# Row scores spread through DRAM, dense jobs paced beside expert pairs, and three norms finished alone

## The chip, the cores and the metric

One core of a Trainium2 chip runs the kernel. The metric is device time in microseconds: the median of the runs of one kernel, each from launch to the end. A profiled execution gives the trace; its span runs from the first to the last instruction.

## The reference, cut to what matters

The input x is 64 batches (graphs) of 256 nodes with 256 features, float32, with one adjacency matrix for all. Two layers follow each other; each is a graph attention and then a feed-forward part, each on the normalised input and added to it:

```python
x = x + elu(gat(layernorm(x), adj, W0, a0))        # 4 heads of 64, slope 0.2
x = x + layernorm(x) @ wf.T + bf
x = x + relu(gat(layernorm(x), adj, W1, a1))       # 1 head of 256, slope 0.01
x = x + moe(layernorm(x))                          # 8 experts, the best 2 of each row

# gat, for one head:
e[i, j] = leaky_relu(s[i] + d[j]);  e[i, j] = -big where adj[i, j] == 0
out = softmax(e) @ h
# moe: logits = t @ router.T; t + sum over the best 2 of weight * (gelu(t @ w1[e] + b1[e]) @ w2[e] + b2[e])
```

The kernel computes exp(leaky_relu(s + d)) as a maximum of two products of exponentials, so an attention matrix costs one VectorE instruction a tile once three numbers a node are known. One of these three is wanted along the free axis, for all partitions alike: the **row terms**. They are found by node on partitions, so they have to be turned and spread.

## The kernel before, in words

**Batches.** `batch_layers` (L594) is a Python generator for one batch; nodes lie on the partitions in two tiles (NT = 2) of 128. It computes the first norm, the first attention, the linear layer, the second attention and the last norm, and the routing logits. Every `yield r` ends its work for this step and gives its rank in the next step; `yield -r` puts it back in the same step at rank r.

**Steps.** The loop at L1241 writes out the whole program in steps. A step takes all active generators from a heap by rank; what they issue stands in that order on each engine's queue. So the order on every engine is fixed when the program is written, and the engines run it in order. A new batch begins every third step (TICKS = 3), so some seven batches are under way at once, each at another place. A step costs no time by itself: it is only an order.

**Row terms of the first attention** (from batch 1 on): `send_terms` (L533) turns them with VectorE (L537), `terms_queue(b).dma_start` (L621) writes 4 KB to DRAM, `spread_terms` (L552, issue at L554) reads them back into all partitions (512 KB), and `scores` (L570) uses them two steps later. The queue is SyncE's (SP) from batch 18 (SETTLED) on.

**Row terms of the second attention**: `projected1` (L497) computes the exponentials `ex` on ScalarE (L511); one step later, at rank 25, `scores1` (L520) has TensorE turn and spread them by two transposes into a PSUM bank `pd` (L523), and VectorE forms the two tiles of `z` (L528). A step after that, at rank 40, `attended` (L576) multiplies (L584).

**Norms.** `norm_stats` (L366) lets VectorE compute means and variances (L378, L379). Two such norms of one step share one finish: the second call does it, or, where there is only one, the end of the step (L1277). `finish_norms` (L399) runs on GpSimd (add, power; L406, L407), and from step 3 * 66 = 198 on (`at_end`) on VectorE, in 11 small instructions (L387 to L404). The norms of the last batches have no partner, for no new batch is loaded.

**Experts.** Batches 0 to 60 are routed: their rows are sent by GpSimd's indirect DMAs (L1066) into regions by expert. A **pair** is 256 rows of one expert. `expert_pair` (L890) loads it (L906 to L935), turns it, computes `hidden` (L964) and `result` (L990), scales it (ScalarE, L961), and `scatter` (L998) adds it to the output by two indirect DMAs of GpSimd (L1004). The two of one pair wait until the two of the pair before have landed (`before`, L1001). There are 129 pairs; from step 165 (SINGLE_AT) on at most one begins in a step.

**Dense jobs.** Batches 61, 62 and 63 are not routed; every expert is applied to all of their rows (`dense_expert`, L1022), in two groups: batch 61 (8 jobs of 1 unit), batches 62 and 63 (8 jobs of 2 units). A unit is one batch under one expert: `hidden` and `product`, then four VectorE instructions (L1036). `dense_free` (L1258 to L1261) spaces the jobs: a job of n units keeps the next one off for n steps. `store_dense` (L1043) writes a batch out when its last job is done.

**Queues.** GpSimd's queue carries the sends, the scatters and the finishes of norms. SP carries all loads, the stores and the row terms. Buffers that bound the run-ahead: 5 of `xr`, 7 of `we` (pairs and dense jobs together), 9 of `y`, 8 PSUM banks, 1 of `z1`.

Of the kernel before, what the change touches and what calls it, by code (L numbers as in the profile page):

```python
# [9 lines left out]
F32 = mybir.dt.float32  # L10
I32 = mybir.dt.int32
AF = mybir.ActivationFunctionType
ALU = mybir.AluOpType
AX = mybir.AxisListType

P = 128
# [5 lines left out]
def rows_to_all(ap: bass.AP, n: int) -> bass.AP:  # L22

    return bass.AP(tensor=ap.tensor, offset=ap.offset, ap=[[0, P], [1, n]])
# [3 lines left out]
def kernel(  # L28
# [17 lines left out]
    nc = tc.nc  # L46
    B, N, D = x.shape
# [4 lines left out]
    NT = N // P  # L52
# [21 lines left out]
    work = ctx.enter_context(tc.tile_pool(name="work", bufs=2))  # L74
    small = ctx.enter_context(tc.tile_pool(name="small", bufs=4))
# [3 lines left out]
    def bank(name, shape):  # L79
        t = psum.tile([P, 2 * D], F32, tag="bank", name=name, bufs=8)  # L80
        n = 1
        for s in shape:
            n *= s
        t = t[:, :n]
        if len(shape) == 2:
            t = t.rearrange("p (a b) -> p a b", a=shape[0])
        elif len(shape) == 3:
            t = t.rearrange("p (a b c) -> p a b c", a=shape[0], b=shape[1])
        return t
# [22 lines left out]
    S = 32  # L112
    G = P // S
# [13 lines left out]
    AHEAD, BLOCKS_AHEAD = 3, 2  # L127
    PAIRED = CHUNKS[0] + CHUNKS[1] + 3
    SETTLED = CHUNKS[0] + CHUNKS[1] + CHUNKS[2] + CHUNKS[3] + 2


    ident = const.tile([P, P], F32, tag="ident", name="ident")
# [186 lines left out]
    def once(work):  # L319
# [14 lines left out]
        out=tri, in_=tri, pattern=[[1, P]], base=0, channel_multiplier=-1,  # L334
# [28 lines left out]
    SINGLE_AT = TICKS * (B - 9)  # L363
    order, order_steps = [], []

    def norm_stats(src):  # L366

        stats = small.tile([P, NT, 6], F32, tag="stats", name="stats")
        if half_done:
            mv, rstd = half_done[0]  # L370
            at = NT
        else:
            mv = small.tile([P, 2 * NT, 2], F32, tag="mv", name="mv", bufs=4)
            rstd = small.tile([P, 2 * NT], F32, tag="rstd", name="rstd", bufs=5)
            half_done.append((mv, rstd))
            at = 0
        for t in range(NT):
            nc.vector.bn_stats(stats[:, t, :], src[:, t, :])  # L378
            nc.vector.bn_aggr(mv[:, at + t, :], stats[:, t, :])  # L379
        if at:  # L380
            finish_norms(2 * NT)
        return mv[:, at : at + NT, :], rstd[:, at : at + NT]

    def at_end():
        return order_steps[-1] >= TICKS * (B + 2)

    def inverse_root(y, v):  # L387

        n = v.shape[-1]
        t = small.tile([P, 2 * NT], F32, tag="root", name="root", bufs=2)[:, :n]  # L390
        nc.vector.tensor_scalar(
            y.bitcast(I32), v.bitcast(I32), -0.5, float(0x5F3759DF), op0=ALU.mult, op1=ALU.add
        )
        for _ in range(3):
            nc.vector.tensor_tensor(t, y, y, ALU.mult)
            nc.vector.scalar_tensor_tensor(t, t, -0.5, v, op0=ALU.mult, op1=ALU.mult)
            nc.vector.scalar_tensor_tensor(y, t, 1.5, y, op0=ALU.add, op1=ALU.mult)

    def finish_norms(n):  # L399
        mv, rstd = half_done.pop()  # L400
        if at_end():
            var = small.tile([P, 2 * NT], F32, tag="sq", name="var", bufs=4)[:, :n]
            nc.vector.tensor_scalar(var, mv[:, :n, 1], EPS, None, op0=ALU.add)
            inverse_root(rstd[:, :n], var)  # L404
            return
        nc.gpsimd.tensor_scalar_add(rstd[:, :n], mv[:, :n, 1], EPS)  # L406
        nc.gpsimd.tensor_tensor(rstd[:, :n], rstd[:, :n], mhalf[:, :n], ALU.pow)  # L407
# [84 lines left out]
    for i in range(2):  # L492
        t = keep.tile([P, NT, D + 1], F32, tag=f"q1_{i}", name=f"q1_{i}")
# [23 lines left out]
            nc.scalar.activation(me[:, j, :], masks[1][:, j, :], AF.Copy, scale=ex[:, j, 0:1])  # L517
        return q, ex, me

    def scores1(ex, me):  # L520
        pd = bank("pd", [N])
        for t in range(NT):
            nc.tensor.transpose(  # L523
                pd[:, t * P : (t + 1) * P], ex[:, t, 1:2].to_broadcast([P, P]), ident
            )
        z = work.tile([P, NT, N], F32, tag="z1", name="z1", bufs=1)
        for j in range(NT):
            nc.vector.scalar_tensor_tensor(  # L528
                z[:, j, :], pd, ex[:, j, 2:3], me[:, j, :], op0=ALU.max, op1=ALU.mult
            )  # L530
        return [z[:, j, :] for j in range(NT)]

    def send_terms(q, b):  # L533


        ut = small.tile([P, S], F32, tag="ut", name="ut", bufs=1)
        nc.vector.transpose(  # L537
            ut.rearrange("p (t h w) -> p t h w", t=NT, h=H), q[:, :, :, HD - 1 : HD + 3]
        )
        ud = tc.dram_tile([S, S], F32, name=f"terms_{b}")  # L540
        ud = ud.rearrange("c r -> (c r)").rearrange("(c p) -> c p", p=P)
        return ut, ud
# [51 lines left out]
    def batch_layers(b, c0, xng, lg):  # L594

        def first_norm():
            x0 = xin.pop(b)
            if b + AHEAD < B:
                xin[b + AHEAD] = load_batch(b + AHEAD)
            return x0, norm_stats(x0)[1]  # L600

        if b:
            x0, rstd = first_norm()
# [8 lines left out]
        if not b:  # L612
            x0, rstd = first_norm()
# [4 lines left out]
        if b:  # L618
            ut, ud = send_terms(q, b)
            yield -31  # L620
            terms_queue(b).dma_start(  # L621
                out=ud.rearrange("c (g r) -> g c r", g=G),
                in_=ut[2 : P : S // (NT * H), :],
            )
            yield -52
        z = work.tile([P, NT, NT, H, P], F32, tag="z4", name="z4", bufs=2)
# [17 lines left out]
        ex = work.tile([P, NT, D], F32, tag="e", name="e", bufs=1)  # L644
        nc.scalar.activation(ex, hp, AF.Exp)

        x1 = work.tile([P, NT, D], F32, tag="x1", name="x1", bufs=1)
# [2 lines left out]
        x1b = work.tile([P, NT, D], F32, tag="x1b", name="x1b", bufs=1)  # L650
        nc.vector.tensor_add(x1b, x1, bias_f[:, None, :].to_broadcast([P, NT, D]))
        yield 21
        _, rstd = norm_stats(x1)
        yield -30
        xT = transposed(x1)
        yield 70
# [9 lines left out]
        for t in range(NT):  # L666
            nc.vector.scalar_tensor_tensor(  # L667
                x2[:, t, :], pf[:, t, :], rstd[:, t : t + 1], x1b[:, t, :],
                op0=ALU.mult, op1=ALU.add, accum_out=sums[:, t : t + 1],
            )  # L670
        yield 7
        rstd = norm_squares(x2, sums)
# [3 lines left out]
        xT = transposed(x2)  # L676
        yield 20
        q, ex, me = projected1(xT, rstd, b)
        yield 25
        z = scores1(ex, me)  # L680
        yield 40
        pvs, rinv = attended(
            q[:, :, None, :], 1, lambda j, h, t: z[j][:, t * P : (t + 1) * P]
# [9 lines left out]
        for t in range(NT):  # L693
            nc.vector.scalar_tensor_tensor(
                x2[:, t, :], x2[:, t, :], 1.0, rel[:, t, :],
                op0=ALU.mult, op1=ALU.add, accum_out=sums[:, t : t + 1],
            )
        yield 6
        rstd = norm_squares(x2, sums)
# [33 lines left out]
        if not dense:  # L733
            d = nc.sync.dma_start(
                out=out_rows[b * N : (b + 1) * N, :].rearrange("(t p) d -> p t d", p=P), in_=base
# [320 lines left out]
    active = []  # L1056
    waiting, dense_jobs = [], []
    sent = []

    def begin(job, rank):  # L1060
        active.append([rank, len(order), job])
        order.append(job)
# [172 lines left out]
    step, more, credit = 2, True, 0.0  # L1235


    SETUP_AT = 4
    dense_free = 0
    with tc.manual_schedule():  # L1240
        while more or active or waiting or dense_jobs or scatters:  # L1241
            phase = step % TICKS
            if more and (phase == 0 or step == 2):
                nxt = next(batches, None)
                more = nxt is not None
                if more:
                    begin(nxt, 40 if phase == 0 else 25)
            if step >= SETUP_AT and setup:
                begin(setup.pop(0)(), 90)
            if step >= SINGLE_AT:  # L1250
                if waiting and len(scatters) < 3:
                    begin(waiting.pop(0)(), 90)
            elif phase == 1:
                credit = min(credit + 3.0, 2.0)
                while waiting and credit >= 1.0:
                    credit -= 1.0
                    begin(waiting.pop(0)(), 90)
            if dense_jobs and step >= dense_free:  # L1258
                units, job = dense_jobs.pop(0)
                dense_free = step + units  # L1260
                begin(job(), 90)  # L1261
            if scatters:
                def one():
                    scatter()
                    return
                    yield
                begin(one(), 97)
            order_steps.append(step)
            queue = [(a[0], a[1], a) for a in active]
            heapq.heapify(queue)  # L1270
            while queue:
                *_, entry = heapq.heappop(queue)
                entry[0] = next(entry[2], None)
                if entry[0] is not None and entry[0] < 0:
                    entry[0] = -entry[0]
                    heapq.heappush(queue, (entry[0], entry[1], entry))
            if half_done:  # L1277
                finish_norms(NT)
            if half_squared:
                finish_squares()  # L1280
            active[:] = [a for a in active if a[0] is not None]
            step += 1
# [35 lines left out]
```

## Time and profile before

| | |
|---|---|
| median of 3 runs | 1486.76 us (1486.3 to 1491.11) |
| the profiled execution | 1489.83 us, its span 1488.0 us |
| TensorE matmul, weight loads | 1420.1 us (95%), 1264.0 us (85%) |
| VectorE | 1232.9 us (83%) |
| ScalarE | 1006.5 us (68%) |
| GpSimd | 864.6 us (58%) |
| DMA queues, share of 16 engines | 42.1% hardware (SP), 23.9% software (GpSimd), 2.3% hardware (ScalarE) |
| granted TensorE clock, mean | 0.985 |

The busy time of TensorE is the union of overlapping matmuls: two that follow each other closely are each longer than the distance between their starts. The distance of the starts is what one costs in a full stream. In the timeline each row has its start, its length, engine, line, operation, tiles and count; in brackets stands the idle time before it and what the profile takes for its end. "SPq" is SyncE's queue, "PEld" TensorE's weight loads. A table by window has for each stretch its length, then busy time and instruction count of TensorE matmuls, weight loads, VectorE, ScalarE and GpSimd, then the granted clock, the busy share of the DMA engines and GB/s.

### The profile page before, as it was taken

The page shows a single profiled execution, that of the slowest core. Times are in us where ns is not written, and L with a number is a line of the kernel's source. Part 1 is how long each engine was busy: PE and PEld are TensorE (multiplying, and loading weights), DVE is VectorE, ACT ScalarE, POOL GpSimd, SP SyncE. Part 2 cuts the span into 40 slices and gives each one's busy share as a digit, 9 for nine tenths or more (in the row PEclk, how much of TensorE's full clock was granted, in tenths as well). Part 3 has the DMA queues.
Part 4 walks back from the last instruction along what each step waited for, and adds up shares of the span by engine and source line. Part 5 has one row for each costly group of instructions (what it writes and reads, how often), then busy time and mean ns, then how long its engine had stood idle before and what let it go on. Part 6 is the DMA issues. An engine that isn't in the chain of part 4 may idle for free. (4 is left out here: it accounts for less than half of the span.)

```text
span 1488.0 us, 29865 instructions
## 1 busy us (share of the span) xinstructions
PE 1420.1 (95%) x8138; PEld 1264.0 (85%) x8138; DVE 1232.9 (83%) x4320; ACT 1006.5 (68%) x2389; POOL 864.6 (58%) x851
## 2 busy tenths in 40 slices
PE   6899999999999999999999999999999999899994
PEld 5688888898999999899999989888888888778883
DVE  7689999988898889899888989998888888765442
ACT  1377667577777777777777787777777878643330
POOL 2122446455857676666758585776666668544444
PEclk9899999999999999999999999999999999999998
DMA  4832243567878777787877687768877786988743
GB/s 128 227 98 86 89 130 117 146 172 153 199 171 193 161 177 170 171 185 180 190 156 190 147 193 168 190 164 186 193 158 172 153 173 128 213 201 150 152 66 49
DMA packets 354081, 236.10 MB, mean 159 GB/s; under 512 B 246260, under 2 KB 316156, under 8 KB 353916
## 3 DMA queue, kind: packets, MB, share of 16 engines
q1 hardware_dynamic: 301000, 157.90, 42.1%
q0 software_dynamic: 48864, 66.33, 23.9%
q10 hardware_dynamic: 4052, 9.98, 2.3%
q8 instruction: 67, 1.10, 0.3%
q14 instruction: 98, 0.80, 0.2%
HBM read 146.00 MB, written 88.09 MB: 157 GB/s over the span
## 5 line engine op out<-in xcount | busy, mean ns | idle before, releaser
L1004 POOL DMA_INDIRECT out_dram<-y,xt x258 | 415.6, 1611 | 214.6 <-issue 54.6
L584 PE MATMUL pv<-q,z 128*128 128x65 f32 (+1 forms) x2560 | 363.7, 297 | 0.7 <-DVE z L570 0.3
L584 PEld LDWEIGHTS pv<-q,z 128*128 128x128 f32 x2560 | 331.2, 193 | 13.3 <-DVE z L570 1.3
L1066 POOL DMA_INDIRECT xs<-xng,pos x244 | 256.3, 1050 | 65.2 <-issue 57.7
L983 PE MATMUL py<-w2s,hT 128*128 (+1 forms) x1224 | 282.9, 382 | 4.7 <-ACT hT L974 4.5
L983 PEld LDWEIGHTS py<-w2s,hT 128*128 128x128 f32 x1224 | 229.7, 191 | 37.2 <-ACT hT L974 7.4
L570 DVE SCALAR_TENSOR_TENSOR z<-z,q,mask 128x256 f32<-128x256 f32 x504 | 231.5, 482 | 15.5 <-DMA z<-terms 6.5
L968 PE MATMUL ph<-sT,we 128*128 128x256 f32 x1032 | 241.4, 383 | 1.6 <-DVE sT L117 0.9
L968 PEld LDWEIGHTS ph<-sT,we 128*128 128x128 f32 x1032 | 195.6, 192 | 28.7 <-DVE sT L117 1.4
L961 ACT ACTIVATE y<-y,w 128x256 f32<-128x256 f32 x258 | 113.4, 499 | 119.4 <-DVE y L993 119.2
L459 ACT COPY xT<-pt 128x512 f32<-128x512 f32 x209 | 121.2, 588 | 82.1 <-PE pt L453 80.0
L974 ACT ACTIVATE hT<-ph,we 128x256 f32<-128x256 f32 x306 | 124.1, 472 | 64.1 <-PE ph L968 46.7
L406 POOL TENSOR_SCALAR rstd<-mv 128x4 f32<-128x4 f32 (+1 forms) x66 | 15.9, 240 | 224.8 <-DVE mv L379 175.3
L504 PE MATMUL pq<-wx,xT 128*128 128x259 f32 x512 | 126.5, 390 | 13.9 <-ACT xT L459 13.9
L424 ACT ACTIVATE off<-x,sums 128x256 f32<-128x256 f32 x256 | 129.2, 505 | 9.2 <-DVE x L667 3.3
L993 DVE TENSOR_TENSOR y<-py,b2s 128x512 f32<-128x512 f32 x129 | 86.9, 687 | 56.3 <-PE py L983 44.8
L469 PE MATMUL pq<-wx,xT 128*128 128x268 f32 x512 | 128.1, 394 | 2.4 <-DVE xT L117 1.2
L504 PEld LDWEIGHTS pq<-wx,xT 128*128 128x128 f32 x512 | 96.0, 192 | 33.6 <-ACT xT L459 19.8
L660 PE MATMUL pf<-wfT,xT 128*128 128x256 f32 x512 | 124.2, 386 | 0.0
L469 PEld LDWEIGHTS pq<-wx,xT 128*128 128x128 f32 x512 | 97.9, 192 | 21.7 <-DVE xT L117 1.4
L688 ACT ACTIVATE rel<-pv,rinv 128x256 f32<-128x256 f32 x128 | 54.0, 469 | 82.1 <-DVE rinv L591 81.8
L660 PEld LDWEIGHTS pf<-wfT,xT 128*128 128x128 f32 x512 | 94.9, 196 | 10.6
(170 smaller groups left out, 2355.7 us busy)
## 6 DMA issues: line engine op xcount, KB each, us to landing
we<-wpack SPq DMA_DIRECT2D x145, 288.0 KB
xr<-xs SPq DMA_DIRECT2D x516, 64.0 KB
z<-terms SPq DMA_DIRECT2D x46, 512.0 KB
xin<-in_x_dram SPq DMA_DIRECT2D x64, 256.0 KB
out_dram<-base SPq DMA_DIRECT2D x61, 256.0 KB
xblk<-in_x_dram SPq DMA_DIRECT2D x188, 64.0 KB
z<-terms ACTq DMA_DIRECT2D x17, 512.0 KB
out_dram<-y,xt POOLq DMA_INDIRECT x258
```

Of the source, the lines that this page charges most:

```text
L424: nc.scalar.activation(off, src[:, t, :], AF.Square, bias=sums[:, t : t + 1], scale=-float(D), accum_out=sq[:, at + t : at + t + 1],)
L459: nc.scalar.copy(dst, pt)
L469: nc.tensor.matmul(pq.rearrange("p h c -> p (h c)"), xT[:, k, t * P : (t + 1) * P], wx[:, k, :], start=(k == 0), stop=(k == KT - 1),)
L504: nc.tensor.matmul(pq, xT[:, k, t * P : (t + 1) * P], wx1[:, k, :], start=(k == 0), stop=(k == KT - 1),)
L570: nc.vector.scalar_tensor_tensor(z[:, j, :, h, :], terms, q[:, j, h, HD + 2 : HD + 3], masks[0][:, j, :].rearrange("p (t i) -> p t i", t=N ...
L584: nc.tensor.matmul(pv[:, h, :], z(j, h, t), q[:, j, h, : d + 1], start=(j == 0), stop=(j == NT - 1),)
L660: nc.tensor.matmul(pf[:, t, :], xT[:, k, t * P : (t + 1) * P], wfT[:, k, :], start=(k == 0), stop=(k == KT - 1),)
L968: nc.tensor.matmul(ph[:, f, :], we[:, k * D + f * P : k * D + (f + 1) * P], xT[:, k, :], start=(k == 0), stop=(k == KT - 1),)
L974: nc.scalar.activation(hT[:, f, :], ph[:, f, :], AF.Gelu, bias=we[:, C_B1 + f : C_B1 + f + 1])
L983: nc.tensor.matmul(py[:, t, :], hT[:, f, t * P : (t + 1) * P], w2s[:, e, f * D : (f + 1) * D].rearrange("p e c -> p (e c)"), start=(f == 0 ...
L1004: d = nc.gpsimd.indirect_dma_start(out=out_rows, out_offset=bass.IndirectOffsetOnAxis(ap=xt[:, t, 0:1].bitcast(I32), axis=0), in_=y[:, t, ...
L1066: d = nc.gpsimd.indirect_dma_start(out=xs_d[: E * CAP * PAIR, :], out_offset=bass.IndirectOffsetOnAxis(ap=at, axis=0), in_=xe, in_offset=None,
```

## The change

Three edits in one.

1. From batch 18 on, the row terms of the second attention go the way of the first: VectorE turns them (`turned_terms1`), SP writes 1 KB to DRAM and reads it back into all partitions of `z1` (128 KB), and `scores1` reads them there, over which its last tile is then written. All of the turning is issued in the step of `projected1` (ranks 26, 31, 52), and `scores1` moves from rank 25 to rank 45 of the next step. The two transposes and the PSUM bank are gone for these 46 batches.
2. While a pair waits or is active, a dense job of n units keeps the next off for 1.25 n steps; otherwise for 0.5 n.
3. The norm before the linear layer of batches 61, 62 and 63 is finished at once, and by GpSimd.

```diff
-    def norm_stats(src):
+    def norm_stats(src, alone=False):
...
-        if at:
-            finish_norms(2 * NT)
+        if at or alone:
+            finish_norms(at + NT, alone)
...
-    def finish_norms(n):
+    def finish_norms(n, alone=False):
         mv, rstd = half_done.pop()
-        if at_end():
+        if at_end() and not alone:
...
+    def turned_terms1(ex, b):
+
+        ut = small.tile([P, S], F32, tag="ut1", name="ut1", bufs=1)
+        nc.vector.transpose(
+            ut.rearrange("p (t w) -> p t w", t=NT),
+            ex[:, :, 1:2].to_broadcast([P, NT, S // NT]),
+        )
+        return ut, tc.dram_tile([N], F32, name=f"terms1_{b}")
+
+    def scores1(ex, me, z, spread):
+
+        terms = z[:, NT - 1, :]
+        if not spread:
+            terms = bank("pd", [N])
...
-        _, rstd = norm_stats(x1)
+        _, rstd = norm_stats(x1, b + AHEAD >= B)
...
         q, ex, me = projected1(xT, rstd, b)
-        yield 25
-        z = scores1(ex, me)
+        spread = b >= SETTLED
+        if spread:
+            yield -26
+            ut, ud = turned_terms1(ex, b)
+            yield -31
+            nc.sync.dma_start(
+                out=ud.rearrange("(t g r) -> g t r", t=NT, g=G),
+                in_=ut[0 : P : S // NT, :],
+            )
+            yield -52
+        z = work.tile([P, NT, N], F32, tag="z1", name="z1", bufs=1)
+        if spread:
+            nc.sync.dma_start(out=z[:, NT - 1, :], in_=rows_to_all(ud, N))
+        yield 45 if spread else 25
+        z = scores1(ex, me, z, spread)
...
             if dense_jobs and step >= dense_free:
                 units, job = dense_jobs.pop(0)
-                dense_free = step + units
+                pairs = waiting or any(a[2].__name__ == "expert_pair" for a in active)
+                dense_free = max(dense_free, step - 0.5) + units * (1.25 if pairs else 0.5)
                 begin(job(), 90)
```

More of the change, by code (lines that the diff above doesn't have):

```diff
@@ L518, in projected1 @@
         return q, ex, me
[L520 to L526, printed above, removed]
+    def turned_terms1(ex, b):
[9 more added lines that the diff above has]
+            terms = bank("pd", [N])
+            for t in range(NT):
+                nc.tensor.transpose(
+                    terms[:, t * P : (t + 1) * P], ex[:, t, 1:2].to_broadcast([P, P]), ident
+                )
         for j in range(NT):
             nc.vector.scalar_tensor_tensor(
-                z[:, j, :], pd, ex[:, j, 2:3], me[:, j, :], op0=ALU.max, op1=ALU.mult
+                z[:, j, :], terms, ex[:, j, 2:3], me[:, j, :], op0=ALU.max, op1=ALU.mult
             )
@@ L678, in batch_layers @@
         q, ex, me = projected1(xT, rstd, b)
-        yield 25
-        z = scores1(ex, me)
+        spread = b >= SETTLED
[6 more added lines that the diff above has]
+                in_=ut[0 : P : S // NT, :],
+            )
+            yield -52
[4 more added lines that the diff above has]
+        z = scores1(ex, me, z, spread)
         yield 40
@@ L1238 @@
     SETUP_AT = 4
-    dense_free = 0
+    dense_free = 0.0
     with tc.manual_schedule():
```

## The prediction, as it was put on record

> **What bounds the kernel now.** I read the table by window first, because one share for the whole span hides stages. Columns: matmul, weight load, VectorE, ScalarE, GpSimd, clock, DMA share, GB/s.
>
> ```profile
> 400.00:500.00 100.00, 100.00 (x596) 90.60 (x595) 89.66 (x307) 77.17 (x182) 70.62 (x68) 1.00 0.79 180
> ...
> 1000.00:1100.00 100.00, 95.36 (x549) 84.86 (x549) 85.61 (x310) 75.93 (x166) 64.34 (x60) 1.00 0.80 180
> 1100.00:1200.00 100.00, 99.69 (x567) 88.08 (x565) 86.90 (x313) 79.46 (x173) 68.32 (x61) 1.00 0.77 165
> 1200.00:1320.00 120.00, 107.94 (x552) 92.65 (x553) 95.68 (x440) 84.13 (x196) 80.38 (x71) 0.96 0.81 180
> 1320.00:1440.00 120.00, 120.00 (x558) 105.64 (x557) 62.27 (x153) 46.42 (x109) 52.48 (x35) 1.00 0.74 140
> 1440.00:1488.00 48.00, 26.27 (x116) 21.12 (x114) 14.31 (x30) 6.85 (x16) 20.32 (x13) 0.85 0.38 50
> ```
>
> See three stages. To about 930 us TensorE never pauses: the stage is worth what its instructions cost. To 1200 it is nearly full; to 1320 it has 12 us of gaps. After 1320 it is full again, but the end lies 48 us behind it with TensorE half idle, so something else sets the end. The timeline of the last 120 us shows what:
>
> ```profile
> 1386.27 0.91 ACT L961 ACTIVATE y<-y,w 128x256 f32<-128x256 f32 x2 [1.55 <-DVE y L993]
> ...
> 1412.67 1.56 POOL L1004 DMA_INDIRECT out_dram<-y,xt  x1 [2.95 <-ACT hT L974]
> ...
> 1414.53 1.56 POOL L1004 DMA_INDIRECT out_dram<-y,xt  x1 [0.30 <-ACT y L961]
> ...
> 1418.96 1.56 POOL L1004 DMA_INDIRECT out_dram<-y,xt  x1 [2.87 <-ACT hT L974]
> ```
>
> Counted from the end, the first row scales pair 119 (pairs count from 0) and 1418.96 is its scatter, 32 us after its data were ready. The names in brackets are chance: what it waits for is the landing of the two scatters before it (L1001). A pair takes 1.56 + 0.30 + 1.56 = 3.4 us on GpSimd and a landing of 2.9 to 3.1 us (6.45 us in all) after 1410, and 3.6 to 4.8 us (7.0 to 8.2) at 1320 to 1390, where the DMA engines are 77 to 90% busy. From pair 105 (1317.4) to pair 128 (1478.3) there are 23 such distances of 7.0 us. This chain sets the end; it runs, landing or sends in between, with gaps of little else, from about 1200 us. The chain view of the page names TensorE (L983, L968) up to 1439; I don't follow it, for the reason just given.
>
> Last, the piece that is replaced, in the steady stage:
>
> ```profile
> 509.25 0.21 DVE L537 STREAM_TRANSPOSE ut<-q 128x32 f32<-128x32 f32 x1
> ...
> 509.49 0.54 SPq L621 DMA_DIRECT2D terms<-ut  x1
> ...
> 511.07 0.38 PE L523 MATMUL pd<-ident,ex 128*128 128x128 f32 x2
> ...
> 511.23 0.35 SPq L554 DMA_DIRECT2D z<-terms  x1
> ...
> 511.29 3.68 PE L584 MATMUL pv<-q,z 128*128 128x65 f32 x32
> ...
> 514.14 0.83 DVE L528 SCALAR_TENSOR_TENSOR z<-pd,ex,me 128x256 f32<-128x256 f32 x2
> ```
>
> **What the Trainium skill says.** "TensorE: Matmul & The Clock Gate", Part 4: PE-mode transpose, gives some 275 ns for a 128x128 transpose inside a kernel; the group row has 278. But its Back-to-back issue gap says that spacing counts, and the trace has it: the next matmul starts 0.22 us after the first of two (511.07 to 511.29). So 0.11 us each, not 0.28. "VectorE: DVE Perf Modes", The three transpose paths: VectorE turns blocks of 32x32 only; hence the way over DRAM. "DMA: Bandwidth & Descriptors", Two DMAs through the same engine are not ordered: the read must wait for the write's completion; its Anatomy of one DMA puts some 2 us on that. The trace has 1.74 us from L621 to L554 (509.49 to 511.23), up to 2.9 in other batches.
>
> **The change, part by part.**
>
> *Transposes.* 46 batches lose 0.22 us of TensorE each. L523 runs for batches 18 to 48 between 331 and 931 us, in the full stage: 31 x 0.218 = 6.8 us, all on the path. For batches 49 to 59 (to 1188 us) it is 11 x 0.218 = 2.4 us in a stage that is 95 to 99.7% full, half of which I count, 1.2 (bounds 0 and 3.3, as some also wait there for `ex`). For 60 to 63, TensorE has gaps anyhow: 0. A PSUM bank comes free earlier, of use to nobody here as TensorE doesn't wait.
>
> *What takes their place.* VectorE: 46 more turnings, 128x32 like L537, 0.21 us: 9.7 us in all, or 1% of an engine that is 89 to 90% busy in that stage: hidden; without cover it would cost just that. It waits for nothing new: ScalarE's `ex` stands ahead of the `q` of L477, for which L485 already waits, just before. L528 read from SBUF instead of PSUM: L570, the same shape from SBUF, takes 482 against 460 ns: +2 us, hidden likewise.
> SP: two more issues (0.54 and 0.35 us). The write waits for VectorE where SP already waits 7 us a batch (321.8 us in 45 waits at L621), so it is moved past nothing. The read waits for the write's landing; queued behind it are the first attention's own read, the base store and the pair loads. They come 0.6 to 0.9 us later and are used one or two steps (7 to 14 us) later: 0.
> DMA: 128 KB x 46 = 5.9 MB on 236 MB; some 0.7 us each at 180 GB/s: 0, except that it can lengthen a landing.
> The one tight spot: L528 used to start 2.3 to 2.9 us after L554 (514.14 against 511.23), later about 1 us after it. The new read is issued about with L554, 0.2 to 0.5 us later. The 512 KB of L554 take 3.5 to 5.6 us to land, with the first packets after about 1. A quarter of that: 1 + (3.5 to 5.6 - 1) / 4 = 1.6 to 2.2 us, an estimate from these rows. So VectorE waits 0 to 0.5 us in the steady stage and 1 to 1.5 us a batch after 1000 us. What is queued behind on VectorE are the reciprocals L591 and L639; the product they lead to is wanted a step later, and in this cycle VectorE idles 0.8 us before L667 anyway. Taken: 0 before 1000 us; after it, the halving above contains it.
>
> *Norms.* GpSimd finishes batch 61's at 1222.9 to 1224.0, behind two scatters, though VectorE had the variance at 1213; L667 waits for it 3.0 us. At its new place ahead of the sends it comes at some 1216. For batch 63, 2.4 us of VectorE (11 instructions, 1264.6 to 1267.0) become 1.0 us of GpSimd, queued behind pair 98's scatter (to 1265.5): no later than now. Of this, GpSimd's chain gains only what its own waits for those batches' squares (L444: 0.3 and 1.2 us) shrink: 1 us (bounds 0 and 3).
>
> *Dense jobs.* I counted the steps. Pair 128's result is written in step 227 in either kernel. Before, 18 of the 24 units stand ahead of it (steps 209 to 226), after only 14; a unit is 16 matmuls of 0.216 = 3.45 us. So the last pair is ready 4 x 3.45 = 14 us earlier, and 10 units lie behind it instead of 6: with 3.45 us where two share a step (steps 233, 234) and 4.3 us where one stands alone (as at 1447.5, 1451.9, 1456.1), 39 us. TensorE ends where it did. But pairs are already ready 30 us before their scatter, so readiness buys nothing; it would with a quicker chain. What can help is that pair loads end earlier, 6.2 us a pair instead of 6.9 over 12 steps, 8 us: one or two more of the landings fall into the quiet time, 1 us each. I take 1 us (bounds -1, and 10 should all of ten loaded landings fall from 4 to 3 us). The stores still come before the last scatter. The backlog grows to about seven pairs of nine `y` buffers: no stall.
>
> Sum: 6.8 + 1.2 + 1 + 1 = **10.0 us**. The profiled execution of 1489.83 us (span 1488.0 and 1.8 around it) would be 1479.8; it was 3.1 above the median, so the median goes from 1486.76 to **1477**.
>
> **The rivals.**
> - *The tail gains as well* (12%). With fewer dense weights under way, landings fall to 3 us through the whole tail: 10 more, 1467. For it: landing follows the DMA share. Against: the pair loads, in packets of 256 bytes, are most of that share and are only moved.
> - *Nothing reaches the end* (14%). The scatter chain from 1060 us on keeps a pace of its own (7.3 to 8.5 us), VectorE's waits after 1000 us eat the rest: 1485. Against: the chain starts after the full stage, and shifts with it.
> - *Slower: VectorE becomes the bound* (12%). If the read lands as late as the 512 KB one, 4.6 us after issue, L528 waits 2.2 us; VectorE then has 17.9 + 0.2 + 2.2 = 20.3 us of a 20.0 us cycle. It decides from a wait of 1.9 us on. 42 batches x 0.35 = +15 us: 1500. Against: a quarter of the bytes, and the estimate of 2 us.
> - That the edits don't do what they say I exclude for the transposes; for dense pacing, doing nothing is my forecast.
>
> **Numbers.** Forecast 1477, chance 62%, its own range 1471 to 1482. Measurement tells apart about 0.3%, 4.5 us: faster means below 1482.3. Faster: 62 + 12 = 74%, a little more from the edge of the second rival: 75%. Same: 13%. Slower: 12%. The range 1467 to 1488 holds the forecast, half of the first rival and most of the second.
>
> **What would show it.** Right: 36 rows of transposes into `pd` instead of 128 (18 batches x 2); a cycle of some 19.8 us instead of 20.0 between 400 and 900 us, TensorE still full; scatters of the tail still 6.4 to 8 us apart and waiting for landings. Wrong: VectorE idle before the `z1` instructions by over 1 us a batch with TensorE below 99% before 900 us (slower), or the tail's mean distance below 6.7 us (the first rival).

## The result, and the profile after

The changed kernel takes 1552.45 us (median of 6 runs, 1549.06 to 1555.61) where the kernel before takes 1488.88 us (6 runs, 1486.3 to 1493.08): a ratio of 1.0425, interval 1.0399 to 1.045. It is 63.6 us slower, and outside the range of the prediction. The profiled execution took 1551.7 us, its span 1549.9.

The table by window of the kernel after, for the stretches that were shown of before (columns as there):

```profile
400.00:500.00 100.00, 94.57 (x554) 84.42 (x553) 85.90 (x291) 73.73 (x172) 66.47 (x64) 1.00 0.74 169
...
600.00:700.00 100.00, 94.84 (x557) 84.80 (x557) 86.43 (x296) 71.92 (x170) 64.87 (x62) 1.00 0.77 177
...
1000.00:1100.00 100.00, 89.51 (x489) 78.11 (x488) 82.82 (x300) 68.36 (x154) 62.38 (x59) 0.93 0.73 168
1100.00:1200.00 100.00, 93.01 (x508) 81.41 (x507) 77.35 (x284) 70.93 (x156) 61.54 (x56) 0.96 0.75 161
1200.00:1320.00 120.00, 109.97 (x606) 95.82 (x604) 96.46 (x379) 92.25 (x204) 81.74 (x76) 0.99 0.69 149
1320.00:1440.00 120.00, 110.68 (x492) 94.86 (x492) 73.78 (x294) 56.63 (x138) 58.37 (x45) 0.93 0.87 186
```

Read the first row against the 100.00 of before: in the stage where TensorE never paused, it now pauses 5 us in 100. And look at the third number pair: VectorE was busy 89.66 us, now 85.90. **Every engine is less busy.** No engine has become the bound; they wait for each other in a circle. Which one, the view of waits tells (engine, line, what ended the wait: us in total, times, longest). From the whole span of the kernel after:

```profile
ACT e L656 <- DVE hp L650: 93.1, 45, 4.4
DVE z L539 <- DMA z<-terms: 73.4, 44, 3.8
...
PEld pq L504 <- ACT xT L459: 67.3, 46, 5.0
...
PE pq L504 <- ACT xT L459: 51.1, 37, 4.6
```

Before, the first and the last of these read

```profile
ACT e L645 <- DVE hp L639: 22.6, 31, 3.1
...
PE pq L504 <- ACT xT L459: 13.9, 9, 2.8
```

and there was no wait of VectorE for row terms of the second attention at all. Three engines now wait, some 45 times each, once a batch. (Line numbers of the kernel after: the z1 instructions are L539, `hp` L650, `e` L656, squares L424, gelu L998.)

The timeline of one step puts them in order. First the kernel before, from the copy of `xT` that opens the step on ScalarE:

```profile
509.31 0.60 ACT L459 COPY xT<-pt 128x512 f32<-128x512 f32 x1
...
510.08 0.45 SPq L96 DMA_DIRECT2D xin<-in_x_dram  x1
...
514.14 0.83 DVE L528 SCALAR_TENSOR_TENSOR z<-pd,ex,me 128x256 f32<-128x256 f32 x2
...
514.89 0.30 DVE L591 RECIPROCAL rinv<-pv 128x4 f32<-128x4 f32 x2
515.11 0.74 DVE L639 TENSOR_TENSOR hp<-pv,rinv 128x256 f32<-128x256 f32 x2
...
516.00 0.63 ACT L645 ACTIVATE e<-hp 128x512 f32<-128x512 f32 x1
...
521.98 0.59 ACT L459 COPY xT<-pt 128x512 f32<-128x512 f32 x1
...
523.52 1.92 PE L504 MATMUL pq<-wx,xT 128*128 128x259 f32 x8
```

Then the same step of the kernel after (another batch):

```profile
640.35 0.60 ACT L459 COPY xT<-pt 128x512 f32<-128x512 f32 x1
640.42 0.17 DVE L523 STREAM_TRANSPOSE ut<-ex 128x32 f32<-128x32 f32 x1
...
640.62 0.54 SPq L695 DMA_DIRECT2D terms<-ut  x1
...
641.77 0.44 SPq L96 DMA_DIRECT2D xin<-in_x_dram  x1
...
642.33 0.39 SPq L702 DMA_DIRECT2D z<-terms  x1
...
643.15 0.34 SPq L565 DMA_DIRECT2D z<-terms  x1
...
646.84 1.01 DVE L539 SCALAR_TENSOR_TENSOR z<-z,ex,me 128x256 f32<-128x256 f32 x2 [0.86 <-DMA z<-terms]
...
647.76 0.24 DVE L602 RECIPROCAL rinv<-pv 128x4 f32<-128x4 f32 x2
647.97 0.75 DVE L650 TENSOR_TENSOR hp<-pv,rinv 128x256 f32<-128x256 f32 x2
...
648.75 0.63 ACT L656 ACTIVATE e<-hp 128x512 f32<-128x512 f32 x1 [2.11 <-DVE hp L650]
...
651.80 1.28 ACT L998 ACT_TABLE_LOAD   x1
...
653.09 1.57 ACT L998 ACTIVATE hT<-ph,we 128x256 f32<-128x256 f32 x4
...
654.54 0.60 ACT L459 COPY xT<-pt 128x512 f32<-128x512 f32 x1
...
655.19 1.14 PE L504 MATMUL pq<-wx,xT 128*128 128x259 f32 x4 [0.97 <-ACT xT L459]
```

Follow the brackets. The read (L702) is issued at 642.33, and VectorE can start on it at 646.84, **4.5 us later**. Behind L539 stands `hp`. Counted from the first copy, `hp` comes at 7.62 us instead of 5.80, ScalarE's `e` at 8.40 instead of 6.69, and the second copy of `xT` ends at 14.79 instead of 13.26. In between, ScalarE works off its queue without a pause: squares, a table load, gelu (L424, L998). It can't take the copy first. Before, 0.95 us lay between that copy and the matmuls that need it. Of the 1.53 us by which the copy is later, these cover 0.95; the matmuls start 14.84 us after the first copy instead of 14.21, and TensorE waits 0.97 for them. The two steps don't hold quite the same work: of the 1.82 us by which `hp` is later, 0.86 are the wait for the terms, and 0.71 a wait of VectorE for `py` (L1017) that the step of before doesn't have. How much the terms cost on average is read from the totals and the experiments, not from this step.

The cycle of a batch (the mean distance from one batch's turning for the first attention to the next one's, batches 22 to 46) is 21.17 us instead of 20.01. By batch 49 the kernel is 31 us further behind than at batch 22, by batch 61 another 22, and by the last scatter another 13.

### The profile page after: what moved, and what is told of

It reads as the page before. It is cut to its first block, busy times and chain, and to the rows that moved or that the text cites. A ratio compares the mean times of both kernels' runs of the same rounds, so it can differ in the third digit from the quotient of the medians.

```text
span 1549.9 us, 29825 instructions
## 1 busy us (share of the span) xinstructions
PE 1426.7 (92%) x8046; PEld 1258.8 (81%) x8046; DVE 1240.9 (80%) x4355; ACT 1006.9 (65%) x2389; POOL 873.0 (56%) x853
## 5 line engine op out<-in xcount | busy, mean ns | idle before, releaser
L504 PE MATMUL pq<-wx,xT 128*128 128x259 f32 x512 | 134.3, 407 | 51.3 <-ACT xT L459 51.1
L998 ACT ACTIVATE hT<-ph,we 128x256 f32<-128x256 f32 x306 | 124.2, 472 | 64.8 <-PE ph L992 35.6
L504 PEld LDWEIGHTS pq<-wx,xT 128*128 128x128 f32 x512 | 97.4, 198 | 80.9 <-ACT xT L459 67.3
L424 ACT ACTIVATE off<-x,sums 128x256 f32<-128x256 f32 x256 | 129.3, 505 | 6.4
L1017 DVE TENSOR_TENSOR y<-py,b2s 128x512 f32<-128x512 f32 x129 | 85.5, 684 | 51.1 <-PE py L1007 43.3
L656 ACT ACTIVATE e<-hp 128x512 f32<-128x512 f32 x64 | 40.4, 631 | 116.3 <-DVE hp L650 93.1
L453 PE MATMUL pt<-ident,x 128*128 128x128 f32 x512 | 85.2, 283 | 25.6 <-DVE x L678 25.3
```

Of the source, the lines that this page charges most:

```text
L424: nc.scalar.activation(off, src[:, t, :], AF.Square, bias=sums[:, t : t + 1], scale=-float(D), accum_out=sq[:, at + t : at + t + 1],)
L504: nc.tensor.matmul(pq, xT[:, k, t * P : (t + 1) * P], wx1[:, k, :], start=(k == 0), stop=(k == KT - 1),)
L998: nc.scalar.activation(hT[:, f, :], ph[:, f, :], AF.Gelu, bias=we[:, C_B1 + f : C_B1 + f + 1])
```

## The experiments

They fell on several chips; the kernel before took 1489.8 to 1503.1 us there (medians). So only ratios to its runs in the same series are compared.

**1. Everything but the row terms.** One line: no batch spreads through DRAM. Dense spacing and norms stay changed.

```diff
-        spread = b >= SETTLED
+        spread = False
```

> The changed kernel with the row terms of the second attention turned by TensorE again; dense pacing and the three norms stay. Theory A (VectorE waits for the terms' landing in front of work that ScalarE's queue and then TensorE need): the loss is all in the spread, so 1487 or a little less, 1480 to 1490, with the batch cycle at 20.0 us again between 400 and 900 us. Rival B (pacing and norms cost the tail): 1495 or more.

Measured: 1488.45 us, ratio 0.9995 (0.9975 to 1.0016). Spacing and norms together are worth nothing that can be seen, and the loss lies with the row terms.

**2. The row terms alone.**

```diff
-        _, rstd = norm_stats(x1, b + AHEAD >= B)
+        _, rstd = norm_stats(x1)
...
-                dense_free = max(dense_free, step - 0.5) + units * (1.25 if pairs else 0.5)
+                dense_free = step + units
```

> The row terms over DRAM alone; dense pacing and norms as before. Theory A: 1540 to 1555, the batch cycle at 21.1 us as in the changed kernel. Rival B: 1530 or less, the rest being lost in the tail.

Measured: 1544.17 us, ratio 1.0362 (1.0326 to 1.0398). Nearly all of the loss. The rest, some 0.6%, appears when the spacing and the norms are added to it; the two intervals almost touch.

**3. The z1 instructions later in VectorE's queue.** Rank 62 puts them behind the reciprocals, `hp` and the sum of the second attention (L718). Nothing else is moved; DMAs and turning are as in the change.

```diff
-        yield 45 if spread else 25
+        yield 62 if spread else 25
```

> The changed kernel with the two z1 instructions issued at rank 62 of their step instead of 45, behind the reciprocals, the product hp and the sum x2 on VectorE; the same instructions and transfers otherwise. Theory A: what counts is what stands behind the wait, so VectorE's wait for the terms falls below 0.4 us a batch and TensorE is full again; cycle 19.8 us, 1475 to 1485. Rival C (the added traffic, or SP's or VectorE's added work, costs the time): still over 1530. Rival D (the chain from the terms to the attention itself is too long for a step): still over 1520.

Measured: 1497.78 us, ratio 1.0051 (1.0035 to 1.0068). The view of waits of this kernel, same lines as above:

```profile
PEld pq L504 <- ACT xT L459: 23.2, 19, 4.4
...
ACT e L656 <- DVE hp L650: 17.9, 22, 2.4
...
PE pq L504 <- ACT xT L459: 16.8, 10, 4.0
...
DVE z L539 <- DMA z<-terms: 9.2, 11, 2.2
```

and its table by window:

```profile
600.00:700.00 100.00, 100.00 (x591) 90.67 (x591) 91.54 (x318) 78.52 (x184) 68.36 (x67) 1.00 0.82 191
...
1000.00:1100.00 100.00, 92.50 (x520) 82.11 (x519) 82.14 (x297) 72.80 (x158) 59.61 (x56) 0.98 0.77 173
```

With the same transfers, TensorE is full again, and the cycle is 19.81 us: 0.20 below before. So the DMAs may land as late as they do, if VectorE has other work ahead of them. My expectation was right for this stage only: the kernel as a whole is still not faster than before, where I had expected 1475 to 1485 us. Between 1000 and 1100 us TensorE is busy 92.5 us of 100, where it was 95.4 before.

**4. All the traffic, but nothing waits for it.** The used terms come from TensorE's transposes as before, at rank 45; the turning, the write and the read go on, into a tile that is not read. The second tile of scores is therefore written over `me`, the masked exponentials.

```diff
-                z[:, j, :], terms, ex[:, j, 2:3], me[:, j, :], op0=ALU.max, op1=ALU.mult
+                (z, me)[j][:, j, :], terms, ex[:, j, 2:3], me[:, j, :], op0=ALU.max, op1=ALU.mult
...
-        return [z[:, j, :] for j in range(NT)]
+        return [(z, me)[j][:, j, :] for j in range(NT)]
...
-        z = scores1(ex, me, z, spread)
+        z = scores1(ex, me, z, False)
```

> The changed kernel with turning, write and read as they are, but the terms that are used come from TensorE's transposes again (the second tile of the scores is written over the masked exponentials, as the spread terms land where it was); nothing waits for the landing. Theory A: 1480 to 1492. Rival C: as slow as the changed kernel, over 1535, as all of the traffic, SP's issues, VectorE's turning and the rank of 45 are there.

Measured: 1494.88 us, ratio 1.0035 (1.002 to 1.005), TensorE at 100% from 400 to 900 us. This is a little above the 1480 to 1492 that I expected. Turning, issues, bytes and the rank of 45 cost some 5 us together (0.2 to 0.5%), and none of it in the full stage, where the cycle is 20.01 us as before. The other 58 us come only when VectorE waits for the landing.

**5. What sets the landing.** SP issues a load of `x` (L96, 256 KB) just ahead of the small read, and the 512 KB read of the first attention (L565) just behind it. The first kernel moves the load behind both reads, the second the small read behind the large one.

```diff
-            if b + AHEAD < B:
+            if b + AHEAD < B and (b < SETTLED):
                 xin[b + AHEAD] = load_batch(b + AHEAD)
...
             x0, rstd = first_norm()
+            if SETTLED <= b < B - AHEAD:
+                yield -75
+                xin[b + AHEAD] = load_batch(b + AHEAD)
             yield 99
```

```diff
-            yield -52
+            yield -54
```

> The changed kernel, with the 256 KB load of x (L96) issued behind both reads of row terms instead of just ahead of them. Theory (the small read shares the DMA engines with what was issued just ahead of it; 256 KB at some 200 GB/s are 1.3 us): issue to start of z1 falls from 4.5 to about 3.3 us, and the loss of 63 us to some 20 to 35: 1510 to 1525. Rival (the 512 KB read and the pair loads issued behind it delay it, or its landing is a fixed latency): no change, 1545 to 1555.

> The changed kernel, with the 128 KB read for z1 issued behind the 512 KB read of the first attention instead of ahead of it. Theory (the landing of that read sets the cycle through VectorE's and ScalarE's queues): landing 0.5 to 2 us later, in 42 batches a further 20 to 80 us: 1575 to 1630. Rival (the two share the engines anyway, whichever is first): 1550 to 1560. If the cycle weren't set by this landing at all: 1545 to 1555.

Measured: 1529.78 us, ratio 1.0256 (1.0229 to 1.0282), and 1633.31 us, ratio 1.0954 (1.0924 to 1.0983). Both move as the landing theory has it, though the gain of the first is smaller than was expected, and the second lies just above its range. From the two traces, the view of waits from 400 to 900 us; first the load moved behind:

```profile
DVE z L539 <- DMA z<-terms: 17.8, 22, 1.5
```

then the read moved behind:

```profile
DVE z L539 <- DMA z<-terms: 61.7, 22, 3.6
```

and the kernel after, between them:

```profile
DVE z L539 <- DMA z<-terms: 32.8, 22, 2.3
```

Set against the cycle of batches 22 to 46 (500 us hold 24.4, 21.6 and 23.6 of them), with 19.81 us (experiment 3) as what it is without the wait:

| kernel | issue of read to start of z1, median of batches 18 to 48 | wait a batch | cycle | above 19.81 |
|---|---|---|---|---|
| load of x behind | 3.55 us | 0.73 us | 20.47 us | 0.66 us |
| after | 4.54 us | 1.39 us | 21.17 us | 1.36 us |
| small read behind | 5.32 us | 2.86 us | 23.14 us | 3.33 us |

In these three, each microsecond of VectorE's wait lengthens the cycle by about one. (In the third kernel TensorE's granted clock is 0.95 to 0.98 in this stage, in the other two 1.00; up to 0.7 of its 3.33 us can come from that, an estimate from the clock and the cycle.) What stands ahead of the small read in SP's queue is in its landing: with the 256 KB behind it z1 starts 1.0 us sooner, with both the 256 KB and the 512 KB ahead of it 0.8 us later. (In the last case the read is also issued about 0.5 us later, which adds to the wait.) The Trainium skill says it so: "DMA: Bandwidth & Descriptors", Queues, rings and completion order, has each DMA engine take descriptors in ring order, and the increment of a semaphore land only after every earlier write of that engine. The 1.0 and 0.8 us agree with this; they don't tell it from a mere sharing of the engines' bandwidth.

**6. Which of the instructions behind the wait matters.** Rank 55 puts z1 directly behind `hp`, still ahead of L718.

```diff
-        yield 45 if spread else 25
+        yield 55 if spread else 25
```

> The changed kernel with the z1 instructions at rank 55 instead of 45: behind the two reciprocals and the product hp of the first attention (1.0 us of VectorE), still ahead of everything else that stood behind them. Theory (what costs is hp, late behind the wait, and behind it ScalarE's e, gelu and copy of xT; nothing else that is queued behind on VectorE): most of the 63 us are gone, 1495 to 1505, like e3_late. Rival (VectorE's queue as a whole loses the time of the wait, less the 1.0 us by which the instructions come later): about half of the loss stays, 1520 to 1535.

Measured: 1533.19 us, ratio 1.0194 (1.015 to 1.0238). My expectation fell: half of the loss stays, as the rival had it. The view of waits from 400 to 900 us shows the new way:

```profile
ACT off L424 <- DVE x L718: 12.4, 11, 1.6
...
DVE z L539 <- DMA z<-terms: 8.7, 11, 1.3
```

`hp` is no longer late, but the sum L718 is, and ScalarE's squares (L424) wait for it; they too stand ahead of gelu and of the copy. TensorE still waits at L504 (29.4 us in 33 waits over the whole span). So it is not one instruction: whatever VectorE owes ScalarE from behind the wait holds ScalarE's whole queue. That this goes on to TensorE through the copy is read off the timeline; no run takes the copy alone out of the queue. VectorE's own wait is only 0.36 us a batch here (8.7 us over 24.4 batches), and the cycle is 20.53 us, 0.72 above 19.81: the one for one of experiment 5 is no law.

**7. The stage in which it can gain.** Rank 62 again, with the old spacing and norms: once for all batches from 18 on, and once for batches 18 to 48 alone.

```diff
-        spread = b >= SETTLED
+        spread = SETTLED <= b < 49
```

> Rank 62 as in e3_late, all batches from 18 on, but with the old spacing of dense jobs and the old norms. In e3_late some 12 us went in the tail, though e1_no_spread, with the new spacing and no row terms over DRAM, lost none. If it is the new spacing together with the row terms that lengthens the tail: 1484 to 1488. If it is the row terms of the last batches alone: 1496 to 1499, like e3_late.

> Row terms over DRAM for batches 18 to 48 only, with the z1 instructions behind the second attention's neighbours on VectorE (rank 62 instead of 45), and with the old spacing of dense jobs and the old norms. Theory (the transposes are worth 0.22 us of TensorE a batch where it is full, the wait for landing is what costs, and after 1000 us there is nothing to gain): 31 x 0.2 = 6 us faster than before, 1482 to 1484. Rival 1 (what TensorE gains in the full stage is given back later whatever happens later, since the scatter chain keeps its own pace): 1487 to 1490. Rival 2 (the added DMAs and turnings cost by themselves): slower than before, 1492 or more.

Measured: all batches 1496.98 us, ratio 1.003 (1.0014 to 1.0047); batches 18 to 48 alone 1486.46 us, ratio 0.9976 (0.9959 to 0.9992), faster than before by 0.24%. The only difference between them is the last 15 batches, and it is 0.54%, 8 us. The table by window of the first, then of the second:

```profile
1000.00:1100.00 100.00, 90.22 (x507) 79.48 (x506) 80.97 (x293) 73.13 (x161) 60.49 (x56) 0.98 0.78 173
```

```profile
1000.00:1100.00 100.00, 95.44 (x551) 84.87 (x550) 84.84 (x307) 75.14 (x163) 62.98 (x59) 1.00 0.78 177
```

5 us of TensorE in one stretch, where its granted clock is lower too (0.98 against 1.00). So from batch 49 on the way over DRAM costs even at rank 62, and the old spacing doesn't cure it: I had suspected the new spacing of lengthening the tail in experiment 3, and this run (1.003 against 1.0051, overlapping intervals) doesn't bear that out. What the trace of the first does show is that rank 62 no longer lies behind the landing there. The same line of its view of waits, from 400 to 900 us, then from 900 to 1300 us:

```profile
DVE z L539 <- DMA z<-terms: 2.6, 6, 0.7
```

```profile
DVE z L539 <- DMA z<-terms: 8.4, 9, 2.4
```

That this wait is what costs the 8 us is not shown.

**8. The load of x moved, with the late rank.** The edit of experiment 5 on both kernels of experiment 7, and on the kernel before.

> As e6_late_oldpace (rank 62, all batches from 18 on, old spacing and norms), with the load of x behind both reads as in e7_xin_behind. e6_late_oldpace loses some 10 us between batch 49 and the tail. If that is the landing (VectorE waits for it at rank 62 too, where batches follow less evenly after 1000 us): about half or more of it is gone, 1486 to 1491. If it comes from rank 62 itself or from the turning and the traffic of the last batches: 1495 to 1498.

> As e5_late_window (batches 18 to 48 only, rank 62, old spacing and norms), with the load of x behind both reads. In the full stage nothing waits for the landing at rank 62 any more, so an earlier landing buys nothing: 1483 to 1487, the same as e5_late_window. If moving the load costs the first norm of a later batch: 1490 or more.

> The kernel before (row terms of the second attention by TensorE in every batch, old spacing and norms) with nothing changed but the load of x behind the 512 KB read of row terms. It tells where the 0.4% come from by which e10_late_xin and e11_window_xin stand better against the kernel before than e6_late_oldpace and e5_late_window do. If the place of this load is worth something by itself: ratio 0.994 to 0.997. If it is worth something only to the small read: 0.999 to 1.001.

Measured: all batches 1503.37 us, ratio 0.999 (0.9972 to 1.0008); batches 18 to 48 1494.21 us, ratio 0.9933 (0.9908 to 0.9958); kernel before with the load moved 1494.87 us, ratio 0.9964 (0.9947 to 0.9981). As a ratio, the first falls where I expected it if the landing were the loss, but by chance: between 900 and 1300 us its VectorE still waits 9.2 us for the terms. I expected nothing of the move in the second, and it gained. The third says why both went so: the place of this load is worth 0.36% by itself, whatever becomes of the small read. The two gains add up (0.9976 x 0.9964 = 0.9940). The second kernel is the fastest of all, 0.67% below the kernel before. What the load stood in the way of I can't say: the trace of the third, from a slower chip than that of before, shows no single wait of before that is gone, and its cycle of batches 22 to 46 is 20.24 us, not shorter than 20.01.

## Why the prediction was wrong, step by step

*Transposes, -8.0 us: right in the full stage.* 36 rows of transposes into `pd` are left instead of 128, and where nothing waits for the landing, the cycle is 0.20 us shorter (experiment 3) against 0.218 foretold. In batches 18 to 48 alone it brings 0.24%, 4 us of a foretold 6.8; the interval (0.08 to 0.41%) holds up to 6. The 1.2 us from later batches didn't come.

*Turnings, issues, bytes, 0 us: right in the full stage.* Experiment 4 puts them at some 5 us, later on.

***The tight spot, "taken: 0": here it failed, in two places.***
1. The size. I scaled the landing of the 512 KB read by bytes: 1 + a quarter of the rest = 1.6 to 2.2 us. It was 4.5. A transfer isn't alone: I had left out the 256 KB issued 0.56 us ahead of it on the same queue (L96), though the trace of before shows that load in the same place, between L621 and L554 (510.08). That is 1.0 us of the error. The scaling itself was wrong as well, for without this load the read still took 3.55 us to its use: by the packet records of that trace the first of its 128 packets starts 1.0 us after the issue, as I had assumed, but the last ends at 3.2 (medians of 31 reads). Why a quarter of the bytes takes so much more than a quarter of the time, no run shows. The time at which VectorE's queue arrives there, 2.3 to 2.9 us after the issue, was about right: it is 2.94 in the kernel after (start of z1 less the idle time before it, median of batches 18 to 48). So VectorE waits 1.39 us a batch in the full stage, not 0 to 0.5.
2. The cover. I wrote that what is queued behind are L591 and L639, and that "the product they lead to is wanted a step later". The product is, but `e` and, by the sum L694, the squares are wanted by ScalarE at once, and behind these in its queue stand gelu and the copy that TensorE needs in this same step. The deadline of a late instruction isn't that of its own result; it is that of everything behind its readers. The cover there, that is the time by which the copy may be late without harm, is 0.95 us in the step shown; yet the batches of the three kernels of experiment 5 pay the wait nearly one for one. Why the cover saves so little is not shown.

*After 1000 us, "the halving contains it": wrong too.* In the kernel after, 12 batches from 49 on lose 22 us, 1.9 each. Not all of this need be waiting as such: between 1000 and 1200 us TensorE's granted clock was 1.00 before, and is 0.93 and 0.96 after, which is worth up to 11 us of full speed in these 200 us (an estimate from the two rows). No run parts the two. From 400 to 900 us the clock is 1.00 in both kernels, so the loss of the full stage has nothing to do with it. Even with rank 62 the last 15 batches cost 8 us.

*Norms and dense jobs, -2 us: nothing* (experiment 1: 0.9995). The forecast that the spacing does next to nothing was right; the 1 us each can't be told from 0.

*The slower rival (1500, 12%)* had the right trigger, a read that lands as late as the large one, and the wrong mechanism. It let VectorE become the bound, and only from a wait of 1.9 us on. VectorE was busy 86%, its wait in the full stage was 1.39 us a batch, below that threshold, and the loss was four times its 15 us. Adding up the busy time and the waits of one engine doesn't bound a loss that goes round through three queues. My own mark for being wrong, VectorE idle before z1 by over 1 us a batch with TensorE below 99%, is what came.

*The first rival ("the tail gains as well")* was answered with a wrong reading: in the trace of before, packets of 256 bytes took 26% of all packets' time between 1320 and 1390 us, not most of it. Nothing hung on it.

*Open:* what the last batches lose by at rank 62, the wait that is left or something else; how much of the loss after 1000 us is the lower clock; whether spacing and row terms together cost 0.6% at rank 45; what moving the load of `x` frees.

## What to carry to other kernels

When a wait enters an in-order queue, walk on: what stands behind it, who reads that, and what stands behind those readers on their own queues, until an engine that is full is reached; the smallest slack on that walk is the most that can be covered, not the time to the deadline of the result itself. Put work that waits for a landing behind the work that other engines are about to need. Count a landing with all that is issued just ahead of it on its queue, not by its own bytes.

## What the runs showed of the hardware that was not expected

A 128 KB read into all partitions took 4.5 us from issue to use behind a 256 KB load, 3.55 us with that load behind it, and 5.3 us behind both the 256 KB load and the 512 KB read: the neighbours on the queue move its landing by up to 1.8 us. Moving one 256 KB load behind one 512 KB read in SP's queue was worth 0.36% (0.19 to 0.53%) of a kernel of 1500 us.
